# A graph network's attention layer: the row of s2 by way of DRAM, v W out of PSUM in one operation, scores two ticks later

## The chip, the cores and the metric

The kernel runs on one core of a Trainium2 chip. The time is the device time of one execution in microseconds (us), as the median of several runs. One further execution was taken by the profiler; all durations below are from it.

## The reference, cut to what matters

64 graphs of 256 nodes with 256 features. A gated graph network of three rounds, a layer norm, and then one graph attention layer with a layer norm. The change lies in the attention layer:

```python
Wh = jnp.matmul(h, W)                     # h: 64 x 256 x 256
s1 = jnp.einsum('bnf,f->bn', Wh, a1)
s2 = jnp.einsum('bnf,f->bn', Wh, a2)
e = jax.nn.leaky_relu(s1[:, :, None] + s2[:, None, :], negative_slope=0.2)
attn = jax.nn.softmax(jnp.where(adj > 0, e, NEG_INF), axis=2)
x = _layernorm(x + jnp.matmul(attn, Wh))
```

For each node n the scores are s1 of n, one number for a row, plus s2 of all 256 nodes, one number for a column.

## The kernel before, in words

**Tiling.** Two graphs are one pair; there are 32 pairs. A pair's 512 nodes are four chunks (k = 0 to 3) of 128 partitions: k // 2 is the graph (g), k % 2 the chunk in it (c). Three pairs are under way at a time: a block is one round of one pair (`blocks`, line 857), and in a turn of three blocks a new pair does round 0, the one before it round 1, the one before that round 2. Attention of a pair runs beside the blocks of the pairs that follow it.

**What sets the order.** The program is written out in an order made by hand. A clock counts ticks; `at(t, step)` (line 89) puts a step on a list, and `product` (line 472), which issues the matmuls of a block, calls `tick()` between them, which issues all steps that are due. A block is 12 ticks, a turn 36. Each engine takes its instructions in that order: TensorE (PE), VectorE (DVE), ScalarE (ACT), GpSimd (POOL), and SyncE (SP), which issues nearly all DMAs.

**A block** (`gates`, line 468): for each half e of the features the products r, n, z and t, each into two PSUM banks `pga` and `pgb` (line 480). ACT takes `pga` out (485, 487), DVE adds `pgb` (489). Sigmoids and the tanh run on ACT (498), and n * r (512), n + t (516), h - n (506) and its product with z (507) on POOL. PSUM is a ring of eight banks: a bank is written again when the tile that held it eight allocations before has been read.

**Ahead of a block** (`front`, line 394): h is cut into pieces `hH` (132, ACT), `hL` (135, POOL), `hD` (138, DVE); the aggregate over the neighbours, `pa` (448, PE, eight matmuls for each half d), from `hi` and `lo`; and its pieces `aH` (132), `aL` (135), `aD` (138). For most pairs `hi` and `lo` of rounds 1 and 2 come from `h_turned` (line 316): a DMA transpose, four gathers `second_h` (314), `V` put together by ACT and DVE (298), `hi` (338, ACT), `lo` (135, DVE).

**Attention** (`attention`, line 558, pairs 0 to 28; t is the tick at the end of the pair's round 2):

- `project(k)` (593, matmuls at 601): chunk k of v W together with s1 and s2 as columns 256 and 257, into a PSUM bank `pwh`.
- `spread(k)` (604): three writes out of that bank, each scaled by the row's norm: s1 (one column), s2 (one column spread over 128 columns, into `sc`), v W (256 columns). Chunks 0 and 1 on ACT (610), 2 and 3 on DVE (612), at ticks 38, 39, 40, 41.
- `rows` (617, tick 42): four transposes on PE (620) of the spread s2, into a bank `s2`, so that each partition holds the row of s2.
- `scores` (622, tick 43): four activations on ACT (624) from that bank into `sc`, with s1 as bias.
- the mask (637, DVE, tick 41), the predicated copy (643, DVE, tick 44), the maximum (645, DVE, tick 45), the exps (648, ACT, ticks 46 and 47).
- `turn_weights(g)` (659, ticks 50, 51): DMA transposes of the exps into `eT`; `gather_weights(g)` (671, ticks 52, 53): eight gathers back into `sc`; `join_weights(g)` (675, copies at 678 on ACT, ticks 56, 57); `combine(g)` (680, matmuls `po` at 685, ticks 58, 59); the norm and the store of `out`.

ACT loads a table ahead of the exps and another after them (ACT_TABLE_LOAD).

`attention_last` (line 707) does the same for the last three pairs, by another timetable; the diff leaves it alone.

Of the kernel before, what the change touches and what calls it, by code (L numbers as in the profile page):

```python
# [9 lines left out]
F32 = mybir.dt.float32  # L10
# [5 lines left out]
AF = mybir.ActivationFunctionType  # L16
ALU = mybir.AluOpType
AX = mybir.AxisListType

P = 128  # L20
NEG_INF = -9000000000000000.0
ALPHA = 0.2
# [5 lines left out]
def kernel(  # L28
# [37 lines left out]
    nc = tc.nc  # L66
    B, N, D = x.shape
    L = weight.shape[0]
    C = N // P
    G = 2  # L70
    K = G * C
# [8 lines left out]
    work = ctx.enter_context(tc.tile_pool(name="work", bufs=2))  # L80
    late = ctx.enter_context(tc.tile_pool(name="late", bufs=1))
    far = ctx.enter_context(tc.tile_pool(name="far", bufs=6, space=bass.MemoryType.DRAM))
# [6 lines left out]
    def at(t, step):  # L89
        clock[1] += 1  # L90
        heappush(pending, (t, clock[1], step))
# [14 lines left out]
    def bank(name):  # L106
        return psum.tile([P, 512], F32, tag="bank", name=name)
# [12 lines left out]
    def flat(t):  # L120
        return t.rearrange("p a b -> p (a b)")
# [38 lines left out]
    ident = const.tile([P, P], F32, name="ident")  # L160
# [31 lines left out]
    for i, tag in enumerate(("wh", "v", "v")):  # L192
        if i < 2:
            w2 = late.tile([P, G, C, D], F32, tag=tag, name=f"w_n{i}", bufs=1 + i)
        t = w2[:, i // 2]
# [77 lines left out]
    def room(kind, shape, p, name=None):  # L273


        name = f"{name or kind}_{p}"
        if p < NP - 3 or p == NP - 3 and kind == "vT":
            return late.tile(shape, F32, tag=kind, name=name, bufs=2 if kind == "v" else 1)
        if p == NP - 3:
            pool, tag, bufs = {"v": (io, "x", 1), "wh": (work, "A", 3), "sc": (work, "hT", 4)}[kind]  # L280
            return pool.tile(shape, F32, tag=tag, name=name, bufs=bufs)
        tag = {"v": "hH", "vT": "hD", "wh": "aH", "sc": "aD"}[kind]
        return work.tile(shape, F32, tag=tag, name=name)
# [27 lines left out]
    def gather(dst, src):  # L311
        for h in range(2):
            for b in range(2):
                nc.sync.dma_start(dst[b * 64:b * 64 + 64, h], src[h::2, :, b])
# [243 lines left out]
    def attention(p, t):  # L558

        s = pairs[p]  # L560
        pts = {}
# [30 lines left out]

        def project(k):
            if k == 0:
                s.wh = room("wh", [P, G, C, D], p)
                s.sc = room("sc", [P, K, N], p)
                s.s1 = work.tile([P, K], F32, tag="s1", name=f"s1_{p}")
                s.s2 = s.sc[:, :, :P]
            pts[k] = bank("pwh")
            for d in range(C):  # L600
                nc.tensor.matmul(pts[k][:, :D + 2], s.vT[:, d, k * P:(k + 1) * P], gw[:, d, :],  # L601
                                 start=(d == 0), stop=(d == C - 1))

        def spread(k):
            rs = s.rs[:, k:k + 1]
            for dst, src in ((s.s1[:, k:k + 1], pts[k][:, D:D + 1]),
                             (s.s2[:, k, :], pts[k][:, D + 1:D + 2].to_broadcast([P, P])),
                             (s.wh[:, k // C, k % C, :], pts[k][:, :D])):
                if k in (0, 1):
                    nc.scalar.activation(dst, src, AF.Copy, scale=rs)  # L610
                else:
                    nc.vector.tensor_scalar(dst, src, rs, None, op0=ALU.mult)
        for k in range(K):
            at(t + 37 + k // 2 * 2, lambda k=k: project(k))
            at(t + 37 + 1 + k, lambda k=k: spread(k))

        def rows():
            pts[0] = bank("s2")
            for k in range(K):
                nc.tensor.transpose(pts[0][:, k * P:(k + 1) * P], s.s2[:, k, :], ident)  # L620

        def scores():
            for k in range(K):
                nc.scalar.activation(s.sc[:, k, :], pts[0][:, (k // C) * N:(k // C + 1) * N], AF.Prelu,
                                     bias=s.s1[:, k:k + 1], alpha=ALPHA)
        at(t + 42, rows)
        at(t + 43, scores)

        s.nm = work.tile([P, K], F32, tag="nm", name=f"nm_{p}")
        s.sm = work.tile([P, K], F32, tag="sm", name=f"sm_{p}")  # L630
# [10 lines left out]

        def masked():
            nc.vector.copy_predicated(flat(s.sc), flat(s.mask), neg.to_broadcast([P, K * N]))
        at(t + 44, masked)
        at(t + 45, lambda: nc.vector.tensor_reduce(s.nm, s.sc, AX.X, ALU.max, negate=True))

        def exps(k):
            nc.scalar.activation(s.sc[:, k, :], s.sc[:, k, :], AF.Exp, bias=s.nm[:, k:k + 1],
                                 accum_out=s.sm[:, k:k + 1])
        for k in range(K):  # L650
            at(t + 46 + k // 2, lambda k=k: exps(k))

        def divide():

            nc.vector.tensor_mul(s.sm, s.sm, s.rs)
            nc.vector.reciprocal(s.sm, s.sm)
        at(t + 51, divide)

        def turn_weights(g):

            if g == 0:
                s.eT = late.tile([P, G, C, C, P], F32, tag="v", name=f"eT_{p}", bufs=2)
            nc.sync.dma_start_transpose(s.eT[:, g].rearrange("p c j n -> p (c j n)").bitcast(U16)
                                        .rearrange("p (q n) -> p q n", n=P),
                                        s.sc[:, g * C:(g + 1) * C, :].rearrange("p c n -> p (c n)").bitcast(U16))

        def planes(g):
            return s.sc[:, g * C:(g + 1) * C, :].rearrange("p c n -> p (c n)").bitcast(U16).rearrange(
                "p (h m n) -> p h m n", h=2, n=P)

        def gather_weights(g):
            gather(planes(g), s.eT[:, g].rearrange("p c j n -> p (c j n)").bitcast(U16).rearrange(
                "p (m b n) -> p m b n", b=2, n=P))

        def join_weights(g):
            dst = s.eT[:, g].rearrange("p c j n -> p (c j n)").bitcast(U16).rearrange("p (n h) -> p h n", h=2)
            for h in (1, 0):
                ENGINES[("aa", "aa")[g][1 - h]](dst[:, h], planes(g)[:, h].rearrange("p m n -> p (m n)"))

        def combine(g):  # L680
            pts[g] = bank("po")
            for c in range(C):
                for j in range(C):
                    e = s.eT[:, g, c, j, :]
                    nc.tensor.matmul(pts[g][:, c * D:(c + 1) * D], e, s.wh[:, g, j, :],  # L685
                                     start=(j == 0), stop=(j == C - 1))

        def add(g):

            s.o = s.eT.rearrange("p g c j n -> p g c (j n)")  # L690
            for c in range(C):
                k = g * C + c
                nc.vector.scalar_tensor_tensor(s.o[:, g, c, :], pts[g][:, c * D:(c + 1) * D], s.sm[:, k:k + 1],
                                               s.v[:, g, c, :], op0=ALU.mult, op1=ALU.add)
        for g in range(G):
            at(t + 50 + g, lambda g=g: turn_weights(g))
            at(t + 52 + g, lambda g=g: gather_weights(g))
            at(t + 56 + g, lambda g=g: join_weights(g))
            at(t + 58 + g, lambda g=g: combine(g))
            at(t + 59 + g, lambda g=g: add(g))  # L700
# [198 lines left out]
    for n, (p, i) in enumerate(blocks):  # L899
        if n + 1 < len(blocks):  # L900
            np_, ni = blocks[n + 1]
            if ni == 0:
                if np_ < FROM:
                    after(1, lambda p=np_: begin(p))
                after(1, lambda p=np_: take_x(p))
                after(2, lambda p=np_: ones(p))
                nxt = np_ + 1
                if nxt < FROM:
                    after(7, lambda p=nxt: load_x(p))
                elif nxt < NP:  # L910
                    later = {}
                    after(26, lambda p=nxt, d=later: d.update(f=x_turned(p)))
                    after(30, lambda d=later: d["f"]())
                    after(33, lambda p=nxt: x_joined(p))
                    after(33, lambda p=nxt: load_x(p))
                after(5 if nxt < FROM else 34, lambda p=nxt: load_adj(p))
            front(np_, ni, clock[0], 
                  CLOSE if n and np_ == blocks[n - 1][0] else
                  EARLY if np_ < FROM and not ni else (FIRST, SECOND, THIRD)[ni])
        gates(p, i, (2, 3, 5) if n + 2 >= len(blocks) or blocks[n + 2][0] == p else (2, 5, 9))  # L920
        if i == L - 1:
            if p < NP - len(LAST):
                attention(p, clock[0])
            else:
                attention_last(p, clock[0], LAST[p - NP])
        elif FROM <= p and p + i + 1 < NP:
            h_turned(p, i, clock[0])
# [32 lines left out]
```

## Time and profile before

| what | value |
|---|---|
| time, median of 3 runs | 2077.53 us (2075.09 to 2078.1) |
| span of the profiled execution | 2073.7 us |
| granted TensorE clock, mean | 0.996 |
| busy: PE, DVE, ACT, POOL | 2045.1, 1786.0, 1659.6, 1615.7 us |
| from one pair's s2 transposes to the next pair's | 62.38 us in 24 of 28 cases |
| transposes of s2 (620) | 116, 17.4 us busy |
| writes of `spread` on ACT (s1, s2, v W) | 258, 373, 488 ns each |
| writes of `spread` on DVE (s1, s2, v W) | 209, 342, 475 ns each |
| scores (624) | 516 ns each |
| exps (648) | 500 ns each |

"Busy" is the time in which an engine had an instruction at work; "span" runs from the first to the last instruction. In the timelines, an entry in brackets is idle time of the engine ahead of the instruction, and what ended it. Where ACT and DVE instructions follow each other closely, one starts up to 0.15 us ahead of the end of the one before. For PE the start of a matmul counts, since matmuls overlap.

### The profile page before, as it was taken

What the parts mean: (1) busy time and instruction counts of PE and PEld (TensorE: products, weight loads), DVE (VectorE), ACT (ScalarE), POOL (GpSimd) and SP (SyncE); (2) the same over time, 40 slices, a digit from 0 to 9 for tenths busy, and PEclk for the clock granted to TensorE, in tenths of its full rate; (3) what the DMA queues carried; (4) which work ended last, traced back from release to release, by engine and by line L of the source; (5) the groups of instructions that cost most, each with busy time, mean ns of one, the idle gap of its engine ahead of it and who ended that gap; (6) DMA issues with size and microseconds to landing.
All of it is one profiled execution on the core that took longest, in us unless ns stands there. A gap on an engine that the chain in (4) does not pass through costs nothing.

```text
span 2073.7 us, 31342 instructions
## 1 busy us (share of the span) xinstructions
PE 2045.1 (99%) x9844; PEld 1721.6 (83%) x9844; DVE 1786.0 (86%) x2896; ACT 1659.6 (80%) x3025; POOL 1615.7 (78%) x1114
## 2 busy tenths in 40 slices
PE   8999999999999999999999999999999999999996
PEld 6888888888888888888888888888888888888884
DVE  6667888889888899888899888899898999888886
ACT  4566788888888888888888888888888888888775
POOL 6788787887787887788887788887788787888762
PEclk9999999999999999999999999999999999999998
DMA  4122466666566666575665575665565675665311
GB/s 132 41 61 61 95 130 140 145 125 146 121 137 135 150 124 145 121 141 131 151 125 137 128 140 132 150 129 133 132 137 132 148 132 130 130 137 134 71 52 61
DMA packets 549733, 254.27 MB, mean 123 GB/s; under 512 B 372608, under 2 KB 541312, under 8 KB 549568
## 3 DMA queue, kind: packets, MB, share of 16 engines
q1 hardware_dynamic: 547776, 250.44, 55.0%
q8 instruction: 78, 1.28, 0.3%
q10 hardware_dynamic: 1616, 1.57, 0.2%
q14 instruction: 87, 0.71, 0.1%
q0 software_dynamic: 176, 0.27, 0.1%
HBM read 69.74 MB, written 33.55 MB: 50 GB/s over the span
## 4 chain that ended last, share of the span: by engine, by line
PE 97%; DVE 1%; ACT 1%; POOL 1%; DMA 0%; issue 0%; POOLq 0%; ACTq 0%; SPq 0%; DVEq 0%
PE pga L480 51%; PE pgb L480 25%; PE pa L448 9%; PE po L685 5%; PE pwh L601 5%; PE s L620 1%; PE pt L378 1%; PE pw L238 0%; PE po L808 0%; DMA rows_hH<-in_L_gnn_w_hh_dram 0%; PE pwh L745 0%; POOL whhL_whh L149 0%; POOL wc0L_wc L149 0%; ACT sc L784 0%; DVE hD L138 0%
## 5 line engine op out<-in xcount | busy, mean ns | idle before, releaser
L506 POOL TENSOR_TENSOR t<-hT,n 128x512 f32<-128x512 f32 x192 | 263.3, 1371 | 189.2 <-ACT n L498 189.1
L516 POOL TENSOR_TENSOR n<-n,t 128x512 f32<-128x512 f32 x192 | 285.5, 1487 | 113.5 <-DVE t L489 103.4
L512 POOL TENSOR_TENSOR n<-n,r 128x512 f32<-128x512 f32 x192 | 316.7, 1649 | 72.9 <-ACT r L498 47.1
L480 PE MATMUL pga<-hH,whhH_whh 128*128 128x512 f32 x1152 | 367.3, 400 | 0.1
L480 PE MATMUL pgb<-hD,whhD_whh 128*128 128x512 f32 x1152 | 356.7, 391 | 0.0
L480 PE MATMUL pga<-hL,whhL_whh 128*128 128x512 f32 x1152 | 356.6, 391 | 0.0
L507 POOL TENSOR_TENSOR t<-t,z 128x512 f32<-128x512 f32 x192 | 271.5, 1414 | 15.1
L135 POOL TENSOR_TENSOR hL<-hT,hH 128x1024 fp32r<-128x1024 f32 x96 | 259.5, 2703 | 3.2 <-ACT hH L132 3.1
L480 PEld LDWEIGHTS pgb<-hD,whhD_whh 128*128 128x128 f32 x1152 | 216.3, 188 | 47.4
L480 PEld LDWEIGHTS pga<-hL,whhL_whh 128*128 128x128 f32 x1152 | 216.2, 188 | 47.2
L480 PEld LDWEIGHTS pga<-hH,whhH_whh 128*128 128x128 f32 x1152 | 208.3, 189 | 36.8 <-ACT r L485 0.9
L138 DVE SCALAR_TENSOR_TENSOR hD<-hH,hT 128x1024 fp32r<-128x1024 f32 x96 | 204.2, 2127 | 0.0
L498 ACT ACTIVATE n<-n,bi 128x512 f32<-128x512 f32 x192 | 138.9, 724 | 75.6 <-POOL n L516 75.3
L519 DVE TENSOR_TENSOR hT<-t,n 128x512 f32<-128x512 f32 x192 | 190.9, 994 | 1.2 <-POOL t L507 1.2
L132 ACT ACTIVATE aH<-pa 128x512 fp32r<-128x512 f32 x192 | 113.9, 593 | 94.4 <-PE pa L448 94.3
L448 PE MATMUL pa<-A,lo 128*128 128x256 f32 x768 | 189.2, 282 | 0.0
L448 PE MATMUL pa<-A,hi 128*128 128x256 f32 x768 | 189.1, 283 | 0.0
L135 DVE TENSOR_TENSOR aL<-pa,aH 128x512 fp32r<-128x512 f32 x192 | 131.0, 682 | 64.9 <-ACT aH L132 64.7
L489 DVE SCALAR_TENSOR_TENSOR r<-pgb,r 128x512 f32<-128x512 f32 x192 | 131.9, 687 | 55.1 <-PE pgb L480 27.1
L485 ACT ACTIVATE r<-pga 128x512 f32<-128x512 f32 x192 | 113.2, 590 | 60.0 <-POOL n L512 34.5
L485 ACT ACTIVATE t<-pga 128x512 f32<-128x512 f32 x192 | 115.5, 601 | 47.0 <-PE pga L480 43.3
L489 DVE SCALAR_TENSOR_TENSOR n<-pgb,n 128x512 f32<-128x512 f32 x192 | 130.8, 681 | 23.7 <-ACT n L487 23.7
(172 smaller groups left out, 5399.4 us busy)
## 6 DMA issues: line engine op xcount, KB each, us to landing
adj<-in_adj_dram SPq DMA_DIRECT2D x64, 512.0 KB, 3.9
second_h<-first_h SPq DMA_DIRECT2D x220, 128.0 KB, 4.1
x<-in_x_dram SPq DMA_DIRECT2D x32, 512.0 KB, 3.8
xT<-hT SPq DMA_DIRECT2D x32, 512.0 KB, 4.5
vT<-xT SPq DMA_DIRECT2D x32, 512.0 KB, 3.8
second<-first SPq DMA_DIRECT2D x116, 128.0 KB, 3.1
second<-v SPq DMA_DIRECT2D x116, 128.0 KB, 3.9
sc<-eT SPq DMA_DIRECT2D x232, 64.0 KB, 2.2
```

The source lines that it names most:

```text
L135: eng.tensor_sub(dst, src, hi.bitcast(F32))
L138: nc.vector.scalar_tensor_tensor(dst, hi.bitcast(F32), 1.0 + U, src, op0=ALU.mult, op1=ALU.subtract)
L448: nc.tensor.matmul(pt[:, g * N:(g + 1) * N], h[:, g * C + c, :], s.A[:, g, c, :], start=(n == 0), stop=(n == len(todo) - 1))
L480: nc.tensor.matmul(pt, w[:, d, o * P:(o + 1) * P], m[:, d, :], start=n in (0, ends + 1), stop=n in (ends, len(todo) - 1))
L485: nc.scalar.activation(dst, a, AF.Copy, scale=1.0 + U)
L489: nc.vector.scalar_tensor_tensor(dst, b, -1.0 / U, dst, op0=ALU.mult, op1=ALU.add)
L498: nc.scalar.activation(dst, dst, func, bias=bias)
L506: nc.gpsimd.tensor_sub(t, h, n)
L507: nc.gpsimd.tensor_mul(t, t, z)
L512: after(2, lambda r=r, n=n: nc.gpsimd.tensor_mul(n, n, r))
L516: after(1, lambda n=n, t=t: nc.gpsimd.tensor_add(n, n, t))
L519: after(lags[2], lambda n=n, t=t, h=h: nc.vector.tensor_add(h, t, n))
```

## The change

`spread` becomes one operation for each chunk, of 258 columns, so that s1 and s2 lie beside v W in one tile; it is on ACT for even chunks and on DVE for odd ones, at ticks 38 and 40. The four transposes go. In their place a DMA writes the column s2 to a scratch tensor in DRAM (128 partitions x 4 single values), and a second one reads it back to all 128 partitions as two rows of 256 values (256 KB), into the places of `sc` where chunk 0 of each graph will stand. Both are issued by SP, at ticks 41 and 42. The scores read that row in SBUF; in each graph chunk 1 is made first and chunk 0 last, over the row itself. The scores come at tick 45 and what follows moves too.

```diff
         def project(k):
             if k == 0:
-                s.wh = room("wh", [P, G, C, D], p)
-                s.sc = room("sc", [P, K, N], p)
-                s.s1 = work.tile([P, K], F32, tag="s1", name=f"s1_{p}")
-                s.s2 = s.sc[:, :, :P]
+                s.whs = room("wh", [P, G, C, D + 2], p)
+                s.wh, s.s1, s.s2 = s.whs[:, :, :, :D], s.whs[:, :, :, D:D + 1], s.whs[:, :, :, D + 1]
...
         def spread(k):
-            rs = s.rs[:, k:k + 1]
-            for dst, src in ((s.s1[:, k:k + 1], pts[k][:, D:D + 1]),
-                             (s.s2[:, k, :], pts[k][:, D + 1:D + 2].to_broadcast([P, P])),
-                             (s.wh[:, k // C, k % C, :], pts[k][:, :D])):
-                if k in (0, 1):
-                    nc.scalar.activation(dst, src, AF.Copy, scale=rs)
-                else:
-                    nc.vector.tensor_scalar(dst, src, rs, None, op0=ALU.mult)
+            dst, src, rs = s.whs[:, k // C, k % C, :], pts[k][:, :D + 2], s.rs[:, k:k + 1]
+            if k % 2:
+                nc.vector.tensor_scalar(dst, src, rs, None, op0=ALU.mult)
+            else:
+                nc.scalar.activation(dst, src, AF.Copy, scale=rs)
         for k in range(K):
             at(t + 37 + k // 2 * 2, lambda k=k: project(k))
-            at(t + 37 + 1 + k, lambda k=k: spread(k))
-
-        def rows():
-            pts[0] = bank("s2")
-            for k in range(K):
-                nc.tensor.transpose(pts[0][:, k * P:(k + 1) * P], s.s2[:, k, :], ident)
+            at(t + 38 + k // 2 * 2, lambda k=k: spread(k))
+
+        def row_out():
+            s.row = far.tile([G, C, P], F32, tag="s2", name=f"s2_{p}")
+            nc.sync.dma_start(s.row.rearrange("g c p -> p g c"), s.s2)
+
+        def row_back():
+
+            s.sc = room("sc", [P, K, N], p)
+            nc.sync.dma_start(s.sc.rearrange("p (g c) n -> p g c n", g=G)[:, :, 0, :],
+                              s.row.rearrange("g c p -> g (c p)").partition_broadcast(P))
 
         def scores():
-            for k in range(K):
-                nc.scalar.activation(s.sc[:, k, :], pts[0][:, (k // C) * N:(k // C + 1) * N], AF.Prelu,
-                                     bias=s.s1[:, k:k + 1], alpha=ALPHA)
-        at(t + 42, rows)
-        at(t + 43, scores)
+            for g in range(G):
+                for c in (1, 0):
+                    nc.scalar.activation(s.sc[:, g * C + c, :], s.sc[:, g * C, :], AF.Prelu,
+                                         bias=s.s1[:, g, c], alpha=ALPHA)
+        at(t + 41, row_out)
+        at(t + 42, row_back)
+        at(t + 45, scores)
...
-        at(t + 44, masked)
-        at(t + 45, lambda: nc.vector.tensor_reduce(s.nm, s.sc, AX.X, ALU.max, negate=True))
+        at(t + 46, masked)
+        at(t + 47, lambda: nc.vector.tensor_reduce(s.nm, s.sc, AX.X, ALU.max, negate=True))
...
-            at(t + 46 + k // 2, lambda k=k: exps(k))
+            at(t + 48 + k // 2, lambda k=k: exps(k))
...
-        at(t + 51, divide)
+        at(t + 52, divide)
...
-            at(t + 50 + g, lambda g=g: turn_weights(g))
-            at(t + 52 + g, lambda g=g: gather_weights(g))
+            at(t + 51 + g, lambda g=g: turn_weights(g))
+            at(t + 53 + g, lambda g=g: gather_weights(g))
             at(t + 56 + g, lambda g=g: join_weights(g))
             at(t + 58 + g, lambda g=g: combine(g))
```

`join_weights`, `combine` and all that follows keep their ticks.

## The prediction

> **What bounds the kernel now.** I read the busy shares first, then the busy time by stretches, then the chain of waits, then the timelines of one pair.
>
> ```profile
> PE 2045.1 (99%) x9844; PEld 1721.6 (83%) x9844; DVE 1786.0 (86%) x2896; ACT 1659.6 (80%) x3025; POOL 1615.7 (78%) x1114
> ...
> PE pga L480 51%; PE pgb L480 25%; PE pa L448 9%; PE po L685 5%; PE pwh L601 5%; PE s L620 1%; PE pt L378 1%; PE pw L238 0%; PE po L808 0%; DMA rows_hH<-in_L_gnn_w_hh_dram 0%; PE pwh L745 0%; POOL whhL_whh L149 0%; POOL wc0L_wc L149 0%; ACT sc L784 0%; DVE hD L138 0%
> ```
>
> ```profile
> 804.79:867.17 62.38, 62.38 (x302) 52.74 (x302) 55.96 (x90) 52.25 (x96) 50.14 (x35) 1.00 0.61 135
> ```
>
> TensorE (PE) is busy for all 62.38 us of a pair's turn; the chain of waits lies on it for 97%. PE never waits here, so PE work that goes is time saved, and work of another engine costs nothing until PE has to wait for it. The question is how near PE already is to waiting. The timelines of the pair whose s2 transposes start at 908.36 answer that; most of the other pairs repeat it to 0.02 us. Columns: start, duration, engine, line, operation.
>
> ```profile
> 907.89 0.63 PE L480 MATMUL pgb<-aD,wc0D_wc 128*128 128x512 f32 x2
> 908.36 0.60 PE L620 MATMUL s<-ident,sc 128*128 128x128 f32 x4
> ...
> 918.00 0.62 PE L480 MATMUL pga<-aL,wc0L_wc 128*128 128x512 f32 x2
> ...
> 930.86 0.28 PE L448 MATMUL pa<-A,lo 128*128 128x256 f32 x1
> ...
> 937.57 1.89 PE L685 MATMUL po<-wh,eT 128*128 128x256 f32 x8
> ```
>
> ```profile
> 914.58 0.69 ACT L487 ACTIVATE n<-pga,bh 128x512 f32<-128x512 f32 x1
> 915.16 0.71 ACT L498 ACTIVATE r<-r,b_sum 128x512 f32<-128x512 f32 x1
> 915.89 1.28 ACT L648 ACT_TABLE_LOAD   x1
> 917.19 0.51 ACT L648 ACTIVATE sc<-sc,nm 128x256 f32<-128x256 f32 x1
> ...
> 919.66 0.58 ACT L485 ACTIVATE t<-pga 128x512 f32<-128x512 f32 x1
> 920.13 0.76 ACT L298 COPY V<-second_h 128x512 uint16<-128x512 uint16 x1
> ...
> 928.29 0.62 ACT L338 CAST hi<-V 128x512 fp32r<-128x512 f32 x1
> ...
> 934.49 0.72 ACT L498 ACTIVATE n<-n,bi 128x512 f32<-128x512 f32 x1 [2.21 <-POOL n L516]
> ...
> 935.68 1.40 ACT L678 COPY eT<-sc 128x512 uint16<-128x512 uint16 x2
> ```
>
> From the exps (917.19) to the second cast `hi` (928.29) ACT has no idle bracket: it is a rigid chain. It feeds PE at two places with little to spare. The subtraction `lo` (DVE, 929.28, 0.68 long) ends at 929.96, and PE loads it as weights 0.11 before its matmul at 930.86: **slack 0.79 us**. The second join of the turned weights ends at 935.68 + 1.40 = 937.08, and PE loads those weights 0.23 before 937.57: **slack 0.26 us**.
>
> **The change part by part.**
>
> *Transposes out.* From `pgb` at 907.89 to the first `pa` at 910.19 pass 2.30 us. That holds eight L480 matmuls, 0.227 each in undisturbed stretches (0.454 per two), so 1.82; the four transposes and the two changes of kind cost 0.48. The chain of waits gives 0.6% of 2073.7 over 29 pairs, 0.43. I take 0.48: 29 x 0.48 = **13.9 us off PE**.
>
> *Spread in one operation.* ACT loses 2 x (258 + 373) ns and DVE 2 x (209 + 342) ns a pair, 1.26 and 1.10 us; two more elements a row are lost in 488 and 476 ns. It goes ahead of the scores, where ACT soon waits for PE anyway (0.56 before `aH` at 911.32, 0.28 before `r` at 912.81), so it moves nothing on PE: nil. The matmuls keep their PSUM banks no longer than before.
>
> *Scores, exps later.* This is the step that counts. In the changed order of ACT, the four scores stand behind the `n` eviction (L487, 914.58 now), not at 909.12; then the `r` sigmoid, then both evictions `z` and `t`, and only then the table load and four exps in a row. So the table load now stands behind the `t` eviction, which has to wait for PE. PE ends that product's `a` part at 918.00 + 0.62 = 918.62, now 0.48 earlier: 918.14. ACT starts 0.10 after such an end (912.71 to 912.81 for `r`): 918.24; + 0.58 = 918.82; + 0.02 and the load's 1.28 = 920.12; four exps at 0.50 (two took 917.19 to 918.19) = 922.12. The V copy, which was at 920.13, starts **2.0 us later**. On DVE the same time comes out: scores from 914.10 + 0.57 = 914.67 for 1.65 (909.12 to 910.77, four; they read SBUF now and not PSUM, where the exps of the same size take 500 ns against 516, so I leave it at that) to 916.32; predicated copy 1.41; `hD` 1.21, which now stands between; maximum 1.21: 920.15.
>
> Behind the V copy ACT's order is unchanged and without idle time, so `hi` goes to 930.3 and ends at 930.9, `lo` ends near 931.6. PE wants it at 930.75 - 0.48 = 930.27: it waits **1.3 us**. The tanh of the same pair (923.83 now) goes to 925.8; POOL, which has waited 2.19 us for it, runs five operations without a gap to 934.45, and ACT's next tanh (934.49) waits for the last. So the second join ends at 939.08, and PE wants it at 937.34 - 0.48 = 936.86: **2.22 us in all**, the first wait contained in it. Net 2.22 - 0.48 = 1.74 us a pair. The last of the 29 has no such block behind it: 28 x 1.74 - 0.48 = **+48.2 us**.
>
> Bounds of that. The five POOL operations took 1.53 + 1.63 + 1.48 + 2.95 + 2.27 = 9.86 there; by their group means (1.371, 1.414, 1.649, 2.703, 1.487) they take 8.62. Then the join asks for 0.98 only, and `lo` sets 1.33: net 0.85 a pair, +23.8 - 0.5 = +23. The values of the spot are nearest, so I keep 2.22.
>
> *The row through DRAM.* No row of the trace shows a 2 KB store of single values or a broadcast load. The r sigmoid ahead of the last spread on ACT (907.55) starts 1.15 earlier without the taken-out writes, so the spread ends near 907.5 and SP issues the store then. Landing times in the DMA table go from 2.2 (`sc<-eT`, 64 KB) to 4.5 (`xT<-hT`) for a store and to 4.9 (`first<-in_x`) for a load. The sum is 4.4 to 9.4 and a little for issuing, so the row is there between 911.9 and 917; ACT comes for it at 914.67. Nearest are the last stores of `out` (3.0, quiet queue) and the loads of `x` (3.8): 914.3. I take no wait; each us beyond costs 28 us, at the far end 2.3 x 28 = +64. A row with four-byte pieces exists, `bi` with 7.6 at the start of the kernel on POOL's queue; with it the row would be 4 us late, and I hold that for unlikely on SP's queue. [...]
>
> *What is queued behind.* SP waits for the spread, then for the store's landing near 910.5. Behind it stand the `vT` load (issued at 904.00 now, used at 921.21) and the four `second_h` gathers (908.91 now, used at 920.13, landing 3.8 after issue): about 911 to 915 and landed near 918.5, before the V copy at 922.1. Hidden; with a store of 7.6 it would not be. The x transposes (2.05) now stand ahead of those of the exps and fill the wait for them; the exps' first transpose goes from 918.31 to 921.3, the second from 921.84 to 922.6. The gathers behind them start 1.7 later (921.3 + 3.7 to land = 925.0, now 923.31), and ACT's demand (930.41) 2.0 later: no further wait counted.
>
> **Rivals.**
> - *The cover holds* (chance 0.12): faster. If ACT gets through with less than 0.26 us of delay against PE, only the transposes count: 2077.5 - 13.9 = 2064. For it: ACT is 80% busy and loses 1.26 us of work a pair. Against it: the `t` eviction cannot start before PE ends, and everything from there to `hi` is without idle time.
> - *Only the V chain stalls* (0.12): POOL catches up: +23, 2101.
> - *The row is late as well* (0.18): the predicated copy on DVE waits for the scores, `hD` behind it, and PE at `hD`: 1 to 2 us more a pair, 2154 to 2182. It decides from a store and load of together 7.2 us.
> - *Gains and stalls cancel* (0.03): 2073 to 2082.
> - *The forecast*, one PE stall of 2.2 us a pair (0.55).
>
> **How the numbers follow.** The profiled execution spans 2073.7 us; the runs' median 2077.53 lies 3.8 above. 2073.7 + 48.2 = 2121.9, + 3.8 = **2126**. The range leaves out the faster case (0.12) and the worst of the late row (0.06): from 2098, below the V chain alone, to 2172, a row 1.6 us late. 0.2% is 4 us, about what a measurement of this kernel can tell from no change: faster 0.12, same 0.03, slower 0.85.
>
> **What would show it.** PE's busy time falls by about 14 us while its idle time grows by some 60, put down to ACT (`hi`, `eT`) and DVE (`lo`) in the waits; the distance between pairs is near 64.1 us, not 61.9; the first exp stands near 920.1 with the `t` eviction ahead of the table load; the row lands within 7 us of the spread. The forecast is wrong if PE does not wait at `pa` and `po`, if the exps start before PE has ended the `t` product, or if scores wait for the row by more than a us.

## The result, and the profile after

The changed kernel takes **2383.21 us** (median of 4 runs, 2382.03 to 2384.57); before, on the same chip, took 2076.75. The ratio is 1.148 (95% interval 1.1466 to 1.1494). The direction was forecast, the size was not: 306 us are lost, and the forecast had 49.

Page of the changed kernel, busy time of the engines and the chain that ended last ("issue" is time in which an engine waited for nothing that the profile shows, "SPq" the time of SyncE's issuing):

```profile
PE 2134.7 (90%) x9728; PEld 1772.9 (74%) x9728; DVE 1846.4 (78%) x2780; ACT 1653.1 (69%) x2909; POOL 1557.9 (65%) x1114
...
PE 44%; DVE 16%; DMA 16%; ACT 11%; issue 6%; SPq 4%; POOL 2%; ACTq 0%; POOLq 0%; DVEq 0%
PE pga L480 22%; PE pgb L480 11%; DMA s<-wh 6%; DMA second_h<-first_h 5%; PE pa L448 4%; PE po L687 4%; DVE lo L135 3%; DMA sc<-s 3%; SPq L314 2%; DVE hT L519 2%; PE pwh L599 2%; ACT L498 1%; DVE n L489 1%; DVE nm L647 1%; DVE z L489 1%
```

PE is busy for 90% of the span, and the chain lies on it for 44% instead of 97%. But PE's busy *time* has grown by 90 us, though 116 transposes are gone. That is the first sign of something besides waiting. Two pairs, by windows (start and end, length, busy time of PE, PEld, DVE, ACT, POOL, then the granted TensorE clock, the DMA engines' busy share and GB/s):

```profile
1088.16:1160.12 71.96, 64.26 (x297) 53.57 (x296) 56.93 (x84) 51.26 (x90) 47.66 (x35) 0.98 0.56 121
1160.12:1234.87 74.75, 66.76 (x298) 55.37 (x297) 58.64 (x87) 52.86 (x94) 48.34 (x35) 0.93 0.53 117
```

About the same matmuls (298) take 64.3 us of work in one pair and 66.8 in the next, at clocks of 0.98 and 0.93; in before it was 62.4 at 1.00. So a pair loses in two ways: PE stands still for some 8 us, and after that it works more slowly. The waits (total us, times, longest):

```profile
ACT sc L625 <- DMA sc<-s: 172.6, 29, 7.3
DVE sc L645 <- ACT sc L625: 172.3, 27, 7.2
...
PE pgb L480 <- DVE hD L138: 156.2, 28, 6.8
...
PE pa L448 <- DVE lo L135: 44.3, 27, 1.7
```

ScalarE waits about 6 us a pair for the row, VectorE's predicated copy as long for the scores, and PE 5.6 us for `hD`, which is queued behind that copy. A second wait, at `pa`, stands apart from it. One pair in the timeline (start, length, engine, line; in brackets the idle time before it and who ended it):

```profile
949.98 0.37 SPq L614 DMA_DIRECT2D s<-wh  x1
...
958.05 0.36 SPq L619 DMA_DIRECT2D sc<-s  x1
...
964.25 1.99 ACT L625 ACTIVATE sc<-sc,wh 128x256 f32<-128x256 f32 x4 [5.80 <-DMA sc<-s]
...
966.27 1.36 DVE L645 COPY_PREDICATED_SCALAR sc<-mask,neg 128x1024 f32 x1 [6.26 <-ACT sc L625]
...
967.53 1.75 DVE L138 SCALAR_TENSOR_TENSOR hD<-hH,hT 128x1024 fp32r<-128x1024 f32 x1
...
969.42 1.19 PE L480 MATMUL pgb<-hD,whhD_whh 128*128 128x512 f32 x2 [5.36 <-DVE hD L138]
...
982.25 0.38 PE L448 MATMUL pa<-A,hi 128*128 128x256 f32 x1 [1.18 <-ACT hi L338]
...
984.28 0.39 PE L448 MATMUL pa<-A,lo 128*128 128x256 f32 x1 [1.65 <-DVE lo L135]
```

The store is issued at 949.98, the load only at 958.05, and the row is there at 964.25: 14.3 us. Until ScalarE came for it at 958.45 only 8.5 had passed. And the two matmuls that follow the wait take 1.19 us, where two such take 0.62 elsewhere. The DMA table gives the size in KB and the median time from issue to landing:

```profile
vT<-xT SPq DMA_DIRECT2D x32, 512.0 KB, 7.3
...
sc<-s SPq DMA_DIRECT2D x29, 256.0 KB, 5.9
...
s<-wh SPq DMA_DIRECT2D x29, 2.0 KB, 8.4
```

A store of 2 KB takes 8.4 us, longer than any load beside it.

### The profile page after: what moved, and what is told of

Its sections match the earlier page's. It is cut to its first block, busy times and chain, and to the rows that moved or that the text cites. A ratio compares the mean times of both kernels' runs of the same rounds, so it can differ in the third digit from the quotient of the medians.

```text
span 2380.2 us, 30686 instructions
## 1 busy us (share of the span) xinstructions
PE 2134.7 (90%) x9728; PEld 1772.9 (74%) x9728; DVE 1846.4 (78%) x2780; ACT 1653.1 (69%) x2909; POOL 1557.9 (65%) x1114
## 4 chain that ended last, share of the span: by engine, by line
PE 44%; DVE 16%; DMA 16%; ACT 11%; issue 6%; SPq 4%; POOL 2%; ACTq 0%; POOLq 0%; DVEq 0%
PE pga L480 22%; PE pgb L480 11%; DMA s<-wh 6%; DMA second_h<-first_h 5%; PE pa L448 4%; PE po L687 4%; DVE lo L135 3%; DMA sc<-s 3%; SPq L314 2%; DVE hT L519 2%; PE pwh L599 2%; ACT L498 1%; DVE n L489 1%; DVE nm L647 1%; DVE z L489 1%
## 5 line engine op out<-in xcount | busy, mean ns | idle before, releaser
L480 PE MATMUL pgb<-hD,whhD_whh 128*128 128x512 f32 x1152 | 386.2, 418 | 156.2 <-DVE hD L138 156.2
L512 POOL TENSOR_TENSOR n<-n,r 128x512 f32<-128x512 f32 x192 | 284.7, 1483 | 270.1 <-ACT r L498 203.2
L480 PE MATMUL pga<-hH,whhH_whh 128*128 128x512 f32 x1152 | 392.0, 424 | 0.0
L480 PE MATMUL pga<-hL,whhL_whh 128*128 128x512 f32 x1152 | 375.3, 408 | 0.0
L480 PEld LDWEIGHTS pga<-hL,whhL_whh 128*128 128x128 f32 x1152 | 233.0, 202 | 53.7
L480 PEld LDWEIGHTS pga<-hH,whhH_whh 128*128 128x128 f32 x1152 | 228.6, 204 | 44.4
L448 PE MATMUL pa<-A,hi 128*128 128x256 f32 x768 | 196.0, 288 | 12.0 <-ACT hi L338 11.6
L448 PEld LDWEIGHTS pa<-A,lo 128*128 128x128 f32 x768 | 148.3, 193 | 54.8 <-DVE lo L135 49.7
L138 DVE SCALAR_TENSOR_TENSOR hD<-hH,hT 128x1024 fp32r<-128x1024 f32 x96 | 187.2, 1950 | 0.0
L645 DVE COPY_PREDICATED_SCALAR sc<-mask,neg 128x1024 f32 x29 | 39.6, 1367 | 186.9 <-ACT sc L625 172.3
L625 ACT ACTIVATE sc<-sc,wh 128x256 f32<-128x256 f32 x116 | 55.7, 504 | 174.5 <-DMA sc<-s 172.6
```

The lines of the kernel that those rows point to most:

```text
L138: nc.vector.scalar_tensor_tensor(dst, hi.bitcast(F32), 1.0 + U, src, op0=ALU.mult, op1=ALU.subtract)
L448: nc.tensor.matmul(pt[:, g * N:(g + 1) * N], h[:, g * C + c, :], s.A[:, g, c, :], start=(n == 0), stop=(n == len(todo) - 1))
L480: nc.tensor.matmul(pt, w[:, d, o * P:(o + 1) * P], m[:, d, :], start=n in (0, ends + 1), stop=n in (ends, len(todo) - 1))
L512: after(2, lambda r=r, n=n: nc.gpsimd.tensor_mul(n, n, r))
```

## The experiments

**The theory** from this profile: two losses that have little to do with each other. The row is late (PE waits at `hD`), and the later ticks cost by themselves (PE waits at `pa`); behind each wait the clock falls. **Rivals:** the row is the whole loss and the order costs the 49 us of the forecast or nothing; the spread or the reading of scores from SBUF is at fault; the half clock has another source than PE's waiting.

The table sums up all runs. "A pair" is the mean distance of one pair's projection to the next over 20 pairs; "idle" is PE's idle time in it; "half" is the time at half clock, and "lost" half of that part of it in which PE worked (what the work would have saved at full clock). All four are in us a pair and worked out from the trace's records.

| kernel | time, us | a pair | idle | half | lost |
|---|---|---|---|---|---|
| before | 2076.75 | 62.41 | 0.01 | 0 | 0 |
| after | 2383.21 | 73.34 | 7.64 | 8.02 | 3.27 |
| e1 row at hand | 2268.51 | 69.39 | 4.63 | 4.95 | 2.22 |
| e2 ticks alone | 2284.60 | 69.97 | 4.62 | 5.12 | 2.34 |
| e3 load does not wait | 2318.82 | 71.05 | 6.24 | 5.46 | 2.31 |
| e4 old ticks, row at hand | 2060.24 | 61.89 | 0 | 0 | 0 |
| e5 spread alone | 2073.96 | 62.35 | 0 | 0 | 0 |
| e6 table load ahead | 2233.08 | 68.27 | 3.48 | 6.83 | 2.68 |
| e7 waits filled | 2215.76 | 67.50 | 0.60 | 0 | 0 |
| e8 row in four pieces | 2235.69 | 68.26 | 3.83 | 4.78 | 2.04 |
| e9 early row, old ticks | 2209.75 | 67.33 | 3.18 | 3.41 | 1.53 |
| e10 hL in four | 2233.47 | 68.27 | 2.92 | 6.83 | 3.09 |
| e11 old ticks, row late | 2454.65 | 75.75 | 10.43 | 10.24 | 2.70 |
| e12 lo and clock mended | 2178.16 | 66.14 | 0.72 | 0 | 0 |

### e1: the row at hand

The changed kernel without store and load; scores read a constant row (a row of W).

```diff
...
-   nc.scalar.activation(s.sc[:, g * C + c, :], s.sc[:, g * C, :], AF.Prelu, ...
+   nc.scalar.activation(s.sc[:, g * C + c, :], gw[:, g, :D], AF.Prelu, ...
...
-        at(t + 41, row_out)
```

> The changed kernel without its two DMAs: the scores read 256 columns of a constant tile in SBUF in place of the row of s2, everything else and all ticks as in the changed kernel (the scores are not the layer's, nothing else is left out). Late-row theory with the forecast's order of the scores: the row was the loss beyond the forecast, so what is left is the forecast's one wait of 2.2 us a pair at the second join: 2126 us, 64.1 us from pair to pair, no PE wait at hD. Late row alone (the order costs nothing): 2064. If the loss lies in something else (the fused spread, the half clock by itself), it stays near 2383.

Measured: 2268.51 us, ratio 1.0926 (1.0908 to 1.0944). Between the theories: the row is 115 us of the loss, and 193 are left without it. PE's wait at `hD` is gone; the one at `pa` for `hi` has grown (66.7 us in all, 11.6 in the changed kernel), the one for `lo` is as long as there (44.0). One thing is peculiar to e1:

```profile
991.54 1.21 DVE L640 TENSOR_REDUCE nm<-sc 128x4 f32<-128x1024 f32 x1
...
992.83 1.28 ACT L643 ACT_TABLE_LOAD   x1 [1.88 <-DVE nm L640]
...
994.12 0.51 ACT L643 ACTIVATE sc<-sc,nm 128x256 f32<-128x256 f32 x1
```

The table load begins only when the maximum has ended, so the exps start 1.3 us later than they need. In the changed kernel it ran ahead: 967.83 to 969.11, while the maximum ended at 970.41. In e1 the 1.88 us of waiting for the maximum stand ahead of the load; in the changed kernel none stands ahead of it, and the exp behind it waits (1.33 us for the maximum). Why the wait stands where it does is not shown. So e1 is not a clean "row in time"; e6 and e8 are.

### e2: the later ticks alone

Before with `scores`, `masked`, the maximum, `exps`, `divide`, `turn_weights` and `gather_weights` at the changed kernel's ticks, and nothing else.

> The kernel before with the later ticks alone: transposes on PE and three writes a chunk kept, scores at 45, predicated copy 46, maximum 47, exps 48 and 49, divide 52, turns 51 and 52, gathers 53 and 54. Order theory of the forecast: exps behind the t eviction, ACT 2.0 us later, slack 0.26: 1.74 us a pair, 2077 + 49 = 2126. Rival (the ticks are innocent, only DMAs hurt): 2077.

Measured: 2284.6 us, ratio 1.101 (1.0993 to 1.1026). The rival that only the row matters falls. e2 is e1 plus the transposes (16 us), with the same waits at `pa` (66.8 and 44.5 us) and the same table load behind the maximum.

### e3: the load does not wait for the store

The changed kernel, but the load reads two rows of the weights, which are always there; the store goes unread.

```diff
-  s.row.rearrange("g c p -> g (c p)").partition_broadcast(P)
+  gat_w[0:G, :].partition_broadcast(P)
```

> The changed kernel with the store still issued, but the load reads two rows of an input in DRAM and so waits neither for the store nor for the spread (the scores are not the layer's). If the store's landing (8 us) is what makes the row late: like the run without DMAs, 2126, and SP is not held. If the load itself or the DMAs beside it are what hurts (the load took 5.9): still over 2200.

Measured: 2318.82 us, ratio 1.1182 (1.1165 to 1.1199). The load waits for no one and is issued at once, and still:

```profile
vT<-xT SPq DMA_DIRECT2D x32, 512.0 KB, 13.1
...
sc<-in_L_gnn_W_dram SPq DMA_DIRECT2D x29, 256.0 KB, 10.9
...
s<-wh SPq DMA_DIRECT2D x29, 2.0 KB, 9.7
```

It lands 10.9 us after its issue, and the `vT` load behind it after 13.1 (3.8 in before). In the pair whose store is issued at 996.90 the last packet of the load is through 5.05 us later, but the load counts as landed only after 9.87, right behind the store (9.68). So in e3 the load was held up behind a store that it does not need: 10.9 us in the median from issue to landing, where the changed kernel's load, issued after the store had landed, took 5.9.

### e4: old ticks, row at hand

e1 with before's ticks: the spread in one operation, no transposes, a constant row in scores.

> The changed kernel without DMAs, constant row in SBUF as scores' input, and the ticks of before (scores 43, predicated copy 44, maximum 45, exps 46 and 47, divide 51, turns 50 and 51, gathers 52 and 53). What the four transposes on PE are worth when nothing else is late: 29 x 0.48 = 13.9 us, 2063. Rival, the order theory with no slack at all (PE only arrives earlier at the same waits, slack 0.26 of 0.48): 29 x 0.26 = 7.5, 2070.

Measured: 2060.24 us, ratio 0.9928 (0.9913 to 0.9943), as the theory had it. One pair by windows:

```profile
955.64:1017.54 61.90, 61.90 (x298) 52.35 (x296) 56.04 (x86) 51.38 (x92) 50.41 (x35) 1.00 0.65 136
```

PE does not wait at all: a pair is shorter by the transposes, 0.52 us.

### e5: the spread alone

Before's ticks and transposes; the spread in one operation, and the transposes take `whs[:, g, c, D + 1:D + 2].to_broadcast([P, P])`.

> Before's ticks and before's transposes; only the spread is the changed kernel's (one operation a chunk into the wider wh), and the transposes take their column from there. All of the computation is in it. Theory (the spread costs nothing and nothing rides on it, because the matmul side never waited for it): 2075, within 5 us of before, and PE's idle time stays at 0.0 a pair; with 2060 for the kernel with old ticks and the row at hand, that puts the whole 15 us of that kernel on the transposes. Rival (the single operation on ScalarE and VectorE frees 8 small operations a pair, and that was part of the 15 us): 2066 to 2070.

Measured: 2073.96 us over 11 runs, ratio 0.9994 (0.9985 to 1.0002). The spread costs nothing and brings 3 us at the most.

### e6: the table load ahead

```diff
+  at(t + 48, lambda: nc.scalar.activation(warm, half, AF.Exp))
```

on top of e1 (constant row). It is a tiny exp that waits for nothing.

> The later ticks with the row at hand (scores read a constant row in place of s2's, nothing stored or loaded), and one tiny Exp of 128x4 put ahead of the four exps, which waits for nothing, so that the activation table is loaded while VectorE still looks for the maximum. Theory (the table load stood behind the wait for the maximum, 1.88 us, and that is part of what makes V, hi and lo late at pa): ScalarE's wait at the maximum shrinks from 1.9 to about 0.6, exps start 1.2 us earlier, the waits at pa fall from 4.1 to about 2.9 us a pair, and the time from 2268.5 to about 2233, or to 2215 if with the shorter wait a half-clock window a pair goes too. Rival (the maximum itself, or VectorE's slow copies beside GpSimd, set the start of what follows): 2262 to 2270.

Measured: 2233.08 us, ratio 1.0757 (1.0741 to 1.0774), the theory's first number.

```profile
977.31 1.28 ACT L645 ACT_TABLE_LOAD   x1
...
978.60 0.20 ACT L645 ACTIVATE warm<-half 128x4 f32<-128x4 f32 x1
...
979.18 0.51 ACT L643 ACTIVATE sc<-sc,nm 128x256 f32<-128x256 f32 x1 [0.38 <-DVE nm L640]
```

The load stands right behind the `t` eviction, and the exps wait 0.38 and not 1.88 + 1.28. PE's idle time falls by 1.15 us a pair.

### e7: the waits filled

e1 (constant row), and in the one `pa` group a pair that waits:

```diff
+  if by_dma and i == 2 and d and not g and n < 2:
+      for m in range((22, 14)[n]):
+          nc.tensor.matmul(pt[:, :N], zero, s.A[:, 0, 0, :], start=(n == 0), stop=(n == 0))
```

> The later ticks with the row at hand (a constant row in scores' place of s2's), and in the one pa group a pair that waits, 22 matmuls of zeros ahead of its first matmul and 14 ahead of its second: PE works through the 2.5 and 1.7 us that it waited in, and nothing of the sums is changed by them. Theory (the half clock comes from PE standing still for 1.9 us or more of a 3.4 us window): the half-clock windows that follow this wait go, PE wins up to 2.2 us a pair, and the time falls from 2268.5 to 2205 to 2225; the matmuls behind the wait take 0.28 again and not 0.41. Rival (the clock falls for another reason, such as load, or the matmuls' own time is not what the loss is made of): unchanged or longer, 2266 to 2275, with the windows still there.

Measured: 2215.76 us, ratio 1.0676 (1.0662 to 1.0691): PE does more and the kernel is 53 us faster.

```profile
1049.59 2.73 PE L452 MATMUL pa<-A,zero 128*128 128x256 f32 x22
1052.27 0.38 PE L453 MATMUL pa<-A,hi 128*128 128x256 f32 x1
1052.49 1.80 PE L452 MATMUL pa<-A,zero 128*128 128x256 f32 x14
1054.33 0.39 PE L453 MATMUL pa<-A,lo 128*128 128x256 f32 x1
1054.56 0.28 PE L453 MATMUL pa<-A,hi 128*128 128x256 f32 x1
```

The granted clock is 1.00 in the pair from 1016.45 to 1083.88 and 0.996 over the run (e1: 0.967), and the matmuls behind the wait take 0.28 again, where e1 had 0.41. So the half clock is here the consequence of PE's standing still; the rival that it comes from something else falls.

### e8: the row in four pieces

The changed kernel whole, with another store: PE turns the four columns of s2 in one transpose, and four lines of 512 bytes are stored, not 512 single values.

```diff
-  nc.sync.dma_start(s.row.rearrange("g c p -> p g c"), s.s2)
...
+  nc.tensor.transpose(pts[0][:K, :P], s.s2.rearrange("p g c -> p (g c)"), ident)
...
+  nc.vector.tensor_copy(lines, pts[0][:K, :P])
+  nc.sync.dma_start(s.row.rearrange("g c p -> (g c) p"), lines)
```

> The changed kernel whole, but the row goes to DRAM in four pieces of 512 bytes and not as 512 single values: PE turns the four columns of s2 in one transpose, VectorE copies them (4x128) out of PSUM, and the store takes them from there. All of the computation is in it. Theory (a store of single values needs 8 us to be complete, though its packets are through in 1.2; a store of long pieces needs 2 to 3): the store lands in about 2.5, the row 5 us earlier, ScalarE's wait for it falls from 5.8 us to about 1.5, and the time from 2383 to 2285 to 2305, near 2268 plus a microsecond a pair. Rival (any store to DRAM with a load behind it takes 8 and 4 us at this place): 2380 to 2390, and the store still lands in 8.

Measured: 2235.69 us, ratio 1.077 (1.0755 to 1.0784), 147.5 us faster than the changed kernel and better than either number (I had counted from e1, which carries its table load). In the timeline no wait for the row is left:

```profile
968.49 0.29 SPq L618 DMA_DIRECT2D s<-lines  x1
...
969.69 0.38 SPq L623 DMA_DIRECT2D sc<-s  x1
...
975.74 1.99 ACT L629 ACTIVATE sc<-sc,wh 128x256 f32<-128x256 f32 x4
```

The load, which waits for the store, is issued 1.2 us after it (8.1 in the changed kernel). This is the changed kernel with its row in time, and it is where the order's own price is to be read. Around `pa` in the same pair:

```profile
991.41 1.27 POOL L512 TENSOR_TENSOR n<-n,r 128x512 f32<-128x512 f32 x1
...
991.60 1.38 DVE L298 COPY V<-second_h 128x512 uint16<-128x512 uint16 x1
992.63 2.55 POOL L135 TENSOR_TENSOR hL<-hT,hH 128x1024 fp32r<-128x1024 f32 x1
...
993.07 0.62 ACT L338 CAST hi<-V 128x512 fp32r<-128x512 f32 x1 [0.97 <-DVE V L298]
...
993.74 0.38 PE L448 MATMUL pa<-A,hi 128*128 128x256 f32 x1 [2.26 <-ACT hi L338]
994.08 1.64 DVE L135 TENSOR_TENSOR lo<-V,hi 128x512 fp32r<-128x512 f32 x1
...
995.78 0.39 PE L448 MATMUL pa<-A,lo 128*128 128x256 f32 x1 [1.65 <-DVE lo L135]
```

VectorE's half of `V` took 0.96 at this place in before and takes 1.38: it starts 0.19 after GpSimd's `n` and ends 0.30 after it. `lo` took 0.68 and takes 1.64: it starts inside `hL` and ends 0.54 behind it (995.18).

### e9: an early row at the old ticks

The one arrangement from which I hoped for less than before: projections and spread early enough for the row to be there at before's ticks, 128 pieces of 16 bytes. All four spreads are on VectorE, and the scores read the row in steps of four values, so it is not the row alone that differs.

```diff
...
+  nc.vector.tensor_copy(s.col, s.s2)
+  nc.sync.dma_start(s.row, s.col)                 # row: [P, G, C]
...
+  nc.sync.dma_start(s.line.rearrange("q p g c -> q (p g c)"), s.row.rearrange("p g c -> (p g c)").partition_broadcast(P))
...
-  at(t + 41, row_out)
-  at(t + 42, row_back)
-  at(t + 45, scores)
+  at(t + 38, row_out)
+  at(t + 39, row_back)
+  at(t + 43, scores)
...
```

> The whole computation, arranged so that the row may be there in time at before's ticks: the four projections go one after another, the spread of all four chunks follows in VectorE's t + 38, the four columns of s2 are put side by side (128x4), stored as 128 pieces of 16 bytes, and loaded back as one line of 2 KB for every partition, which scores reads in steps of four; scores and all behind it stand where they stood in before, and the transposes are gone. Theory (a store of 512 single values needs 8 us, fewer and longer pieces some 1.5 to 2; and a row that lands before scores costs nothing): the store is seen complete in 2 us or less, the row lands at about scores' start, and the time is 2060 to 2072. Rival (pieces of 16 bytes are as slow as single values): the row is 6 us late, PE waits, and the time is above 2200.

Measured: 2209.75 us, ratio 1.0653 (1.0637 to 1.0669). Neither theory holds as put: the store of 128 pieces takes neither 2 us nor 8.

```profile
L614 SPq DMA_DIRECT2D s<-s x29: 338/339/345, 216.8 to 2099.6; - x29
...
DMA to landing us min/median/max: 1.4/3.6/4.9
```

3.6 in the median, and the load behind it 4.6. ScalarE waits 3.4 us a pair for the row (98.4 over 29), which is more than there is slack.

### e10: hL in four operations

e8, with GpSimd's `hL` of the third layer's blocks in four operations of 256 columns.

```diff
-            lower(nc.gpsimd, flat(s.hc[1]), flat(s.hT), flat(s.hc[0]))
+            for q in range(4 if i == 2 else 1):
+                w = GN * C // (4 if i == 2 else 1)
+                cut = slice(q * w, (q + 1) * w)
+                lower(nc.gpsimd, flat(s.hc[1])[:, cut], flat(s.hT)[:, cut], flat(s.hc[0])[:, cut])
```

> The kernel with the row in four pieces (2235.7), and in the blocks of the third layer GpSimd's hL, one operation of 2.5 us over 1024 columns, is four operations of 256 columns. All of the computation is in it. Theory (a VectorE operation from SBUF to SBUF that starts beside a GpSimd operation ends only when that operation has ended, so that lo waits for hL's end): lo takes 0.8 to 1.2 and not 1.64, PE's wait at lo falls from 1.56 to about 1.0, and the time to 2217 to 2226. Rival (the two engines merely share a path at a lower rate for as long as both work, or hL is not what lo waits for): lo still 1.5 or more, 2232 to 2240.

Measured: 2233.47 us, ratio 1.0766 (1.0748 to 1.0784). The mechanism came out as the theory had it, the time as the rival:

```profile
1057.39 4.44 POOL L135 TENSOR_TENSOR hL<-hT,hH 128x256 fp32r<-128x256 f32 x4
...
1058.52 0.42 PE L451 MATMUL pa<-A,hi 128*128 128x256 f32 x1 [2.26 <-ACT hi L338]
1058.85 0.71 DVE L135 TENSOR_TENSOR lo<-V,hi 128x512 fp32r<-128x512 f32 x1
...
1059.62 0.58 PE L451 MATMUL pa<-A,lo 128*128 128x256 f32 x1 [0.68 <-DVE lo L135]
```

`lo` takes 0.71, PE waits 0.68 for it, and PE's idle time falls by 0.91 us a pair. The half clock takes back 1.05 (lost: 2.04 to 3.09): it now lasts 6.83 us a pair and no longer 4.78. So `lo` did wait for `hL`'s end, and the gain was eaten by the clock.

### e11: the row late at the old ticks

The changed kernel with before's ticks.

> The changed kernel whole, but scores and all behind it at before's ticks: the row goes and comes as in the change, single value by single value. Theory (the row needs its 14 us whatever the ticks are, and ScalarE, standing at scores, holds up everything behind it): ScalarE waits 9 to 11 us a pair for the row and not 5.8, PE loses as much as in the changed kernel or more, and the time is 2370 to 2420; the later ticks hid nothing that counts. Rival (the later ticks are the cost themselves, and the row's lateness is mostly hidden): 2230 or less.

Measured: 2454.65 us, ratio 1.1831 (1.1813 to 1.1848), above the range expected. ScalarE waits 13.2 us a pair for the row:

```profile
ACT sc L625 <- DMA sc<-s: 383.9, 29, 14.9
```

I had counted two ticks as 4.8 us. By the trace ScalarE comes for the row 10.8 us behind the pair's first projection and not 16.9 as in the changed kernel, and the row lands 24.2 us behind it and not 22.9 (the store goes out a us later). The two make 7.4 us, about the whole of the 7.3 by which the wait has grown. With e4, e8 and after this makes a square: with the row in time the later ticks cost 175 us (2060 to 2236; 173 to e6, which like e4 has a constant row and no store), with the row late they save 71 (2455 to 2383).

### e12: lo and clock mended

e10 with 18 and 5 matmuls of zeros in the two waits, as in e7.

> The kernel with the row in four pieces and hL in four (2233.5), with 18 matmuls of zeros ahead of the first matmul of the pa group that waits and 5 ahead of its second, so that PE works through most of the 2.3 and 0.65 us that it waited in; the zeros change none of the sums. Theory (the order costs three things that add up: the wait proper, lo's extra microsecond behind GpSimd, and the half clock that follows the wait): with the last two gone, the period falls by the 3.1 us a pair that the half clock took there, to about 65.2, and the time to 2140 to 2160. Rival (the period is held by something else, such as the 3.41 us grid that the clock goes by, or a later wait takes back what is won): 2200 or more.

Measured: 2178.16 us, ratio 1.0497 (1.0479 to 1.0514), between the two: 2.13 us a pair of the 3.1 come back.

```profile
1067.61:1133.51 65.90, 65.41 (x322) 55.07 (x321) 56.25 (x86) 51.50 (x91) 48.90 (x38) 1.00 0.63 132
```

The clock is whole. Of the 0.97 us that do not come back, 0.4 are a new wait: PE comes sooner to e8's transpose, and the spread is not ready (10.6 us in 26 waits for ScalarE's `wh`). The zeros (23 of 0.117, 2.7) stand for the order's own waiting. Some 0.6 is left unexplained.

## Why the prediction was wrong, point by point

Two terms of the sum failed. The row was put at no wait, and its store alone took 8.4 us where the sum had 3.0. The order's own wait was put at 2.22 us a pair; it was 3.83, and the half clock that follows it, 2.04 more, had no term (both in e8, where the row is in time).

- **Transposes out, 0.48 us a pair:** right. e4 gives 0.52.
- **The spread, nil:** right. e5 is within the measurement of before.
- **The row, "I take no wait":** wrong, and the largest error. I took 3.0 for the store and 3.8 for the load; they took 8.4 and 5.9. ScalarE comes for the row when it was forecast to (17.1 us behind the pair's first projection, 16.9 measured); it is the row that is late. That scores would wait for the row by more than a us was among the prediction's own signs of being wrong. The rival "the row is late as well" named the way (predicated copy, `hD`, PE) and its turning point, store and load of together 7.2 us; the real 14.3 is twice that, and the cost is not 1 to 2 us a pair but 5.1 (after less e8: 73.34 - 68.26), 147.5 us in the time. The wrong choice was the nearest row: I went by size in bytes and by queue, to large stores of long lines, and set aside `bi` (7.6). It would have given about the right number, though perhaps not for the right reason: `bh` (7.4) and `a_w` (6.8) beside it have four-byte pieces too, but so late is also `gw` (7.3), in pieces of 1 KB. e8 and e9 show that the pieces decide: the same 2 KB in four are stored in at most 1.2, in 128 in 3.6. (e8's store also leaves from 4 partitions and not from 128; e9's does not.)
- **What is queued behind, "hidden":** right, though not for the reason given. A store of 7.6 us was to uncover it; with 8.4 `vT` lands in 7.3 us and not 3.8, and `second_h` in 5.4 and not 4.1, but of all the copies `V` one waits for `second_h`, 0.2 us. The copy that was to come for them at 24.6 us comes at 30.6 (both behind the pair's first projection): it is late by the row as well.
- **"The V copy starts 2.0 us later":** nearly right. The forecast puts that copy 24.6 us behind the pair's first projection (922.1 less 897.55); in e8 it stands at 25.1. The 0.5 come from `hD` ahead of the maximum: 1.76, not 1.21, beside a GpSimd operation. That the table load would not wait for the maximum held in the changed kernel and in e8, and failed in e1 and e2.
- **"Behind the V copy ACT's order is unchanged and without idle time", PE waits 1.3 us at `pa`:** the place was right, the size not. PE waits 2.26 + 1.65 = 3.9 there in e8. I carried over VectorE's durations from before; at the new time three operations start inside others of GpSimd and end behind them: `sm` 0.66 instead of 0.15, `V` 1.38 instead of 0.96, which makes ScalarE wait 0.97 ahead of `hi`, and `lo` 1.64 instead of 0.68. In before `lo` stood beside `hL` as well, but the two started together, and it was `hL` that took longer (2.95, in e8 2.55):

```profile
929.27 2.95 POOL L135 TENSOR_TENSOR hL<-hT,hH 128x1024 fp32r<-128x1024 f32 x1
```

```profile
929.28 0.68 DVE L135 TENSOR_TENSOR lo<-V,hi 128x512 fp32r<-128x512 f32 x1
```

  In e8 `lo` comes 1.45 us into `hL`. e10 took `hL` out of `lo`'s way and so shows this one; `sm` and `V` are read from the timeline only. In the trace of after 56 of the 110 `lo` from `V` start more than 0.1 us into a GpSimd operation; none of them ends before it, and their median is 1.18, against 0.68 for those that start beside none. What makes them last so long no run shows.
- **The second join at `po`, "2.22 us in all":** not reached. PE's wait at `pa` is longer than the join's lateness, and at `po` PE waits for 2.6 us in all at the most (e11). The total idle time in e8 is 3.83.
- **No term for the clock:** in before PE hardly waited between one pair and the next and had a clock of 1.00 there, and I priced waiting at its own length. In e8 the half clock adds 2.04 us a pair, in after 3.27. e7 shows where it comes from.

Together: the forecast had +1.74 us a pair. With the row in time it is +5.85 (e8): idle 3.83 and half clock 2.04, less 0.52 for the transposes; the remaining 0.5, e8's own transpose among it, is not traced. The late row makes it +10.93, and 28 x 10.93 = 306, the measured difference. Of the 110 us by which e8 (2236) misses the forecast (2126), the longer wait makes about 45 (28 x (3.83 - 2.22)) and the clock 57 (28 x 2.04).

**A version better than both** did not come out. e5 is even with before; e4 shows that 15 us would be had if the row came for nothing, and e9, which came nearest to that, is 3.4 us late. That the row can't be had sooner is not shown; the norm's scale, ready about 4 us behind the first projection in before, was the earliest point I used.

## What to carry to other kernels

Price a small store to DRAM by the number and length of its pieces, not by its bytes or its queue (2 KB took 8.4 us in 512 pieces, 3.6 in 128, at most 1.2 in 4), and count what stands behind it in the queue (e3's load: 10.9 us, not 5.9). Where a TensorE that has never waited begins to wait, add the clock's loss to the wait: about half as much again in e8 and after, from a quarter (e11) to as much again (e10) elsewhere. And take a VectorE duration for its place in time only (`lo` took 0.68 in before and 1.64 in e8): where an order moves, look at which GpSimd operation runs there.

## What the runs showed of the hardware

- **A 2 KB store to DRAM, by its pieces:** 512 of 4 bytes 8.4 us (after), 128 of 16 bytes 3.6 (e9), 4 of 512 bytes at most 1.2 (e8). The moving itself is not what takes the time. From the issue at 949.98 to 952 in after all of the store's packets are through, and then there are none until the store is complete (two windows of the DMA view, 949.9 to 952 and 952 to 958):

```profile
DMA packets 529, 0.02 MB, mean 9 GB/s; under 512 B 528, under 2 KB 528, under 8 KB 528
```

```profile
DMA packets 0, 0.00 MB, mean 0 GB/s; under 512 B 0, under 2 KB 0, under 8 KB 0
```

  In the median of the 29 stores of after, the packets begin 0.9 us after the issue and are through at 1.3, and landing follows 7.1 us behind the last; in e9 they begin at 1.9 and are through at 2.4, and landing follows after 1.05. What is waited for in those 6 us no run shows.
- **The half clock, in the trace of after.** Its clock records have 47 stretches at half clock, which begin at multiples of 3.4133 us from one another, to within 0.004; 25 of them last 3.413 us and 21 last 6.827. With the span from 230 to 2300 us cut into windows of 3.413 on the same places, full clock was followed by half clock behind 43 windows, in which PE was idle for 1.65 us or more, and by full clock behind 499, in which it was idle for at most 1.82; between 1.65 and 1.82 both occur. Behind a window at half clock it returned to full in 43 cases, with PE idle in that window for at most 0.52 us, and stayed at half in 21, with 0.68 or more. In e7 and e12, where PE is idle for 0.60 and 0.72 us a pair, the pairs in the windows had a clock of 1.00.
- **A shorter wait that saved no time.** In e6 and e10 a pair takes 68.27 us, which is 20 times the 3.413 of after, in twenty pairs running, to within 0.04, though their idle times differ by half a us (3.48 and 2.92); the half clock lasts 6.83 us a pair in both, twice 3.413. If the clock keeps to 3.413 there as well, the wait lies at the same place of it in every pair; that is my reading.
